# A stack of position-mixing convolutions: fp32 matmuls replaced by products of float32r pieces

## The chip, the cores and the metric

The kernel runs on one core of one Trainium2 chip. The metric is the device time of one execution in microseconds (us); the time of before is the median of three runs. The core has TensorE (PE; its weight loads are listed apart as PEld), VectorE (DVE), ScalarE (ACT), GpSimd (POOL) and SyncE (SP). SP and ACT issue the DMAs here, each in the order of its own queue.

## The reference

A float32 image `x` of shape (4, 32, 32, 16) (batch, height, width, channel) passes through four layers, each added to its input. Layers 0 to 2 are one function with different weights:

```python
def layer(inputs, M, Wp, G):              # inputs = group_norm(x)
    first = einsum('ijpq,bpqc->bijc', M2, inputs)
    shifted = conv3x3(inputs, K)          # K: G as [3, 3, c, (h, w, f)]: own taps for each position (i, j)
    diff = relu(inputs[:, :, :, None, None, :] - shifted)
    second = einsum('ijpq,bpqijc->bijc', W2, diff)
    return first - second
```

For each of the 1024 positions (i, j) a 3x3 convolution of the whole image with 16 input and 16 output channels is computed, subtracted from the image, clipped at zero and summed over the image with the weights `Wp` of that position. Layer 3 is a causal two-dimensional convolution whose impulse response is the inverse DFT of a quotient of two DFTs, made from 8x8 coefficients.

## The kernel before

**Layout.** A position is (cc, p, q) with row 8 cc + p and column q. The pair (cc, q) is a "blk", 128 of them; the eight p and 16 channels make up the 128 partitions. One blk's convolution is a matmul whose 128 outputs are (p, f), whose contraction is (tap, input channel), and whose 512 columns are half of one batch's image. Four batches of 32 x 32 columns are therefore eight such matmuls, taken four at a time (two batches, two halves): the loop `for b0 in (0, 2)` inside `for blk in range(NBLK)`, 256 groups a layer and 768 in all.

**Taps.** The image is normalised (`group_norm`, L82), padded into `ypad`, written to DRAM (`img`, L125, eight DMAs) and read back twelve times with a shift for each tap (`load_patches`, L118; copies on L135). `main` holds taps 0 to 7 on 8 x 16 partitions, so eight taps are one K = 128 matmul (L226). `last` holds tap 8 four times, on 16 partitions of each of the four row tiles of the array, so that the four matmuls of the ninth tap (L235, K = 16) work in four row tiles on four PSUM banks. Everything is fp32.

**Second term.** VectorE reads two PSUM banks at a time, takes the minimum with 0, multiplies by `Wp` and sums along the row in one instruction (L244), two for each group.

**Loads.** `load_g` (L179, ACT's queue) brings G for eight blks at a time (a chunk, 16 a layer): 512 KB for eight taps and four copies of the ninth tap's 64 KB; POOL subtracts the identity at the centre tap (L193). `load_w` (L201, SP's queue) brings 1 MB of Wp for two blks. `load_m` (L141) brings M in four parts of 1 MB for the first term (`first_term`, L146: transposes, 64 matmuls of 64 columns on L159, transposes back).

**PSUM.** Two pools: `ps`, three tiles of two banks for the groups, and `sm`, two single banks for everything else.

**Impulse response.** `impulse_response` (L259) is a generator; layer 0 takes one step of it after each blk (`next(side, None)`), so that its matmuls (L280, L281, L316), its POOL arithmetic (L293 to L304) and its loads lie between the groups of layer 0. Layer 3 then uses the result (L377).

A planner orders each engine's instructions by the dependences and an estimate of when they are ready; each engine runs its own list in order. In the order of before, half of layer 1's and layer 2's first term comes after the first groups of the loop.

Of the kernel before, what the change touches and what calls it, by code (L numbers as in the profile page):

```python
"""Three preactivated position-mixing convolutions and a causal IIR convolution on a (4, 32, 32, 16) image.

Positions.  A position n = (cc * 8 + p) * 32 + q is split into p (8 values) and blk = (cc, q) (128
values).  The residual stream lives in SBUF as [(p, channel), batch, blk].

Layers 0 to 2.  Per position n, s - y is a 3x3 convolution of the normalised image y with
G[n] - (1 at the centre tap).  TensorE computes it for the 8 x 16 (p, f) of a blk at a time, on an image
that holds each tap's shifted copy on partitions of its own: eight taps are one K = 128 matmul, and
the ninth is a K = 16 matmul in one of four row tiles of the array, which work side by side on four
PSUM banks.  VectorE then computes sum_m Wp[n, m] * min(s - y, 0) in one pass over PSUM.  # L10

Layer 3.  The filter's impulse response comes from DFTs as matmuls; the truncated linear
convolution is a block-Toeplitz matmul over (row in block, channel), one for each shift in q and
each block of eight rows, all accumulated in one PSUM bank.
"""
# [8 lines left out]
F32 = mybir.dt.float32  # L24
AF = mybir.ActivationFunctionType
# [8 lines left out]
ROW = B * 34  # one padded image row of all batches  # L34
IMG = 34 * ROW
SPAN = 31 * ROW + 3 * 34 + 32  # what a tap's copy has to hold
GC = 8  # blks per load of G
# [4 lines left out]
TQ = 4  # shifts in q per load of the Toeplitz operand  # L42
# [3 lines left out]
def conv_stack_kernel(ctx, tc, x, M, W, G, den, num, h0, cst, dft, idft, out):  # L46
# [7 lines left out]
    wp = ctx.enter_context(tc.tile_pool(name="wp", bufs=3))  # L54
    gp = ctx.enter_context(tc.tile_pool(name="gp", bufs=2))
    mp = ctx.enter_context(tc.tile_pool(name="mp", bufs=2))
    junkp = ctx.enter_context(tc.tile_pool(name="junk", bufs=2))
    tp = ctx.enter_context(tc.tile_pool(name="tp", bufs=3))
    dram = ctx.enter_context(tc.tile_pool(name="dram", bufs=1, space=DRAM))
    ps = ctx.enter_context(tc.tile_pool(name="ps", bufs=3, space=PSUM))  # L60
    sm = ctx.enter_context(tc.tile_pool(name="sm", bufs=2, space=PSUM))

    def small_psum():
        return sm.tile([P, 512], F32, tag="sm", name="sm")

# [6 lines left out]
    # normalised image with zero columns at the sides, and the zero rows of its copy in DRAM  # L72
    ypad = const.tile([P, 4, B, 34], F32, name="ypad")
    nc.gpsimd.memset(ypad, 0.0)
    zrow = const.tile([C, ROW], F32, name="zrow")
    nc.gpsimd.memset(zrow, 0.0)
    img = dram.tile([C, 34, ROW], F32, name="img")
    nc.scalar.dma_start(out=img[:, 0, :], in_=zrow)
    nc.scalar.dma_start(out=img[:, 33, :], in_=zrow)
    hd = dram.tile([C, C, HLEN], F32, name="hd")  # L80

    def group_norm(xt):  # L82
        """(x - mean) / sqrt(var + 1e-5) over positions and pairs of channels."""
# [18 lines left out]
        # ScalarE's root is short of fp32: one step of Heron's rule after it  # L102
# [15 lines left out]
    def load_patches(y):  # L118
        """[(tap, channel), row, batch, column] of taps 0 to 7, and tap 8 four times over."""
        nc.vector.tensor_copy(  # L120
            ypad[:, :, :, 1:33], y.rearrange("p b (cc q) -> p cc b q", q=S)
        )
        rows = img[:, 1:33, :].rearrange("c (cc p) x -> p c cc x", p=8)
        for p in range(8):
            (nc.sync, nc.scalar)[p % 2].dma_start(  # L125
                out=rows[p],
                in_=ypad[p * C : (p + 1) * C].rearrange("c cc b x -> c cc (b x)"),
            )
        flat = img.rearrange("c r x -> c (r x)")
        main = pp.tile([P, 34, B, 34], F32, tag="main", name="main")  # L130
        last = pp.tile([P, 34, B, 34], F32, tag="last", name="last")
        jobs = [(main, t * C, (t // 3) * ROW + t % 3) for t in range(8)]
        jobs += [(last, g * 32, 2 * ROW + 2) for g in range(4)]
        for n, (to, at, shift) in enumerate(jobs):
            (nc.sync, nc.scalar)[n % 2].dma_start(  # L135
                out=to[at : at + C].rearrange("c r b x -> c (r b x)")[:, :SPAN],
                in_=flat[:, shift : shift + SPAN],
            )
        return main, last

    def load_m(layer, part):  # L141
        mt = mp.tile([P, 2, 8, P], F32, tag="mt", name="mt")
        nc.scalar.dma_start(out=mt, in_=M[layer][:, 2 * part : 2 * part + 2])
        return mt

    def first_term(layer, xt, y):  # L146
        """x + M y, as [(p, c), b, blk]."""
# [6 lines left out]
        for part in range(4):  # L154
            mt = load_m(layer, part)
            for k in range(2):
                pn = 2 * part + k
                for pm in range(8):
                    nc.tensor.matmul(  # L159
                        pf[:, bass.ts(pn, B * C)],  # L160
                        lhsT=mt[:, k, pm, :],
                        rhs=yt[:, pm].rearrange("k b c -> k (b c)"),
                        start=(pm == 0),
                        stop=(pm == 7),
                    )
# [13 lines left out]
    def load_g(layer, ch):  # L179
        g = gp.tile([P, GC, 8, C], F32, tag="g", name="g")  # L180
        g9 = gp.tile([P, GC, 8, C], F32, tag="g9", name="g9")
        cols = bass.ts(ch, GC * P)
        nc.scalar.dma_start(
            out=g.rearrange("r n p f -> r (n p f)"), in_=G[layer][:P, cols]
        )
        for t in range(4):
            nc.scalar.dma_start(
                out=g9[32 * t : 32 * t + C].rearrange("r n p f -> r (n p f)"),
                in_=G[layer][P : P + C, cols],
            )  # L190
        # the centre tap gives s - y in place of s
        mid = g[64 : 64 + C].rearrange("r n p f -> r (n p) f")
        nc.gpsimd.tensor_tensor(  # L193
            mid,
            mid,
            ident[64 : 64 + C, 64 : 64 + C].unsqueeze(1).to_broadcast([C, GC * 8, C]),
            ALU.subtract,
        )
        return g, g9

    def load_w(layer, blk):  # L201
        """Wp's rows of two blks, each on its 16 partitions."""
# [9 lines left out]
    def conv_layer(layer, xt, side=None):  # L212
        y = group_norm(xt)
        main, last = load_patches(y)
        xf = first_term(layer, xt, y)
        acc = work.tile([P, B, NBLK], F32, tag="acc", name="acc")
        for blk in range(NBLK):
            if blk % GC == 0:
                g, g9 = load_g(layer, blk // GC)
            if blk % 2 == 0:  # L220
                wt = load_w(layer, blk)
            n = blk % GC
            for b0 in (0, 2):
                pt = [ps.tile([P, 2, 512], F32, tag="pt", name="pt") for _ in range(2)]
                for t in range(4):
                    nc.tensor.matmul(  # L226
                        pt[t // 2][:, t % 2, :],
                        lhsT=g[:, n].rearrange("r p f -> r (p f)"),
                        rhs=main[:, bass.ts(t % 2, 16), b0 + t // 2, :S],
                        start=True,  # L230
                        stop=False,
                    )
                for t in range(4):
                    rows = slice(32 * t, 32 * t + C)
                    nc.tensor.matmul(  # L235
                        pt[t // 2][:, t % 2, :],
                        lhsT=g9[rows, n].rearrange("r p f -> r (p f)"),
                        rhs=last[rows, bass.ts(t % 2, 16), b0 + t // 2, :S],
                        start=False,
                        stop=True,  # L240
                    )
                for t in range(2):
                    junk = junkp.tile([P, S * S], F32, tag="junk", name="junk")
                    nc.vector.scalar_tensor_tensor(  # L244
                        junk,
                        pt[t].rearrange("p h m -> p (h m)"),
                        0.0,
                        wt[:, blk % 2, :],
                        ALU.min,
                        ALU.mult,  # L250
                        accum_out=acc[:, b0 + t, blk : blk + 1],
                    )
            if side is not None:
                next(side, None)
# [83 lines left out]
    def load_toeplitz(k):  # L338
# [3 lines left out]
        for p in range(8):  # L342
# [3 lines left out]
            )  # L346
        return t

    xs = conv_layer(0, xs, impulse_response())
    xs = conv_layer(1, xs)  # L350
    xs = conv_layer(2, xs)

# [102 lines left out]
```

## Time and profile before

| | us |
|---|---|
| three runs | 3991.12, 3995.35, 4002.98 |
| median | 3995.35 |
| profiled execution, span | 3994.8 |
| TensorE busy | 3884.4 (97%) |
| VectorE busy | 1863.0 (47%) |
| ScalarE busy | 15.3 |
| GpSimd busy | 154.1 |
| DMA | 281.95 MB, mean 71 GB/s |
| mean granted TensorE clock | 0.984 |

Busy times are unions over the span: TensorE's matmuls overlap in its pipeline, so their mean duration (612 ns for a record of L226) is longer than the time from one to the next. In the groups of instructions each line reads: line, engine, operation, output<-inputs, shapes and count; then busy us and the mean ns of one; then the idle time just before them on that engine and what ended most of it. In a timeline a line is: start, duration, engine, line, operation, count, and in brackets the idle time before and what ended it. In a table of stretches each row is the stretch, then busy us (and count) of PE, PEld, DVE, ACT and POOL, the granted TensorE clock, the DMA engines' share and GB/s.

### The profile page before, as it was taken

The page shows a single profiled execution, that of the slowest core. Times are in us where ns is not written, and L with a number is a line of the kernel's source. Part 1 is how long each engine was busy: PE and PEld are TensorE (multiplying, and loading weights), DVE is VectorE, ACT ScalarE, POOL GpSimd, SP SyncE. Part 2 cuts the span into 40 slices and gives each one's busy share as a digit, 9 for nine tenths or more (in the row PEclk, how much of TensorE's full clock was granted, in tenths as well). Part 3 has the DMA queues.
Part 4 walks back from the last instruction along what each step waited for, and adds up shares of the span by engine and source line. Part 5 has one row for each costly group of instructions (what it writes and reads, how often), then busy time and mean ns, then how long its engine had stood idle before and what let it go on. Part 6 is the DMA issues. An engine that isn't in the chain of part 4 may idle for free.

```text
span 3994.8 us, 32173 instructions
## 1 busy us (share of the span) xinstructions
PE 3884.4 (97%) x13092; PEld 1490.9 (37%) x13092; DVE 1863.0 (47%) x3137; ACT 15.3 (0%) x27; POOL 154.1 (4%) x112
## 2 busy tenths in 40 slices
PE   4999999999999899999999999979999999999998
PEld 3333333333333333333333333343333333333335
DVE  0444444444444444444444444434444444444441
ACT  0000000000000000000000000000000000000000
POOL 0300000000000000000000000000000000000000
PEclk9999999999999899999999999979999999999999
DMA  6235322222223432222222222252222222222214
GB/s 157 59 77 104 78 61 69 66 66 69 61 65 74 79 96 66 61 67 67 66 62 69 63 67 71 61 97 61 61 69 67 65 61 69 65 66 70 61 43 69
DMA packets 65186, 281.95 MB, mean 71 GB/s; under 512 B 8173, under 2 KB 26381, under 8 KB 38350
## 3 DMA queue, kind: packets, MB, share of 16 engines
q1 hardware_dynamic: 39806, 218.72, 23.6%
q10 hardware_dynamic: 25232, 61.17, 6.4%
q8 instruction: 102, 1.67, 0.2%
q14 instruction: 46, 0.38, 0.0%
HBM read 277.43 MB, written 2.43 MB: 70 GB/s over the span
## 4 chain that ended last, share of the span: by engine, by line
PE 96%; DMA 4%; DVE 0%; issue 0%; POOL 0%; SPq 0%; ACT 0%; ACTq 0%; POOLq 0%; DVEq 0%
PE pt L226 71%; PE pt L235 21%; PE sm L377 2%; DMA last<-img 1%; DMA w<-in_W_dram 1%; PE sm L316 1%; PE sm L159 1%; DMA table<-in_dft_dram 1%; DMA main<-img 0%; DMA tb<-in_idft_dram 0%; PE sm L280 0%; DVE junk L244 0%; PE sm L281 0%; DMA g<-in_G_dram 0%; DMA img<-ypad 0%
## 5 line engine op out<-in xcount | busy, mean ns | idle before, releaser
L226 PE MATMUL pt<-main,g 128*128 128x512 f32 x6144 | 2888.2, 612 | 48.1 <-DMA last<-img 47.9
L244 DVE SCALAR_TENSOR_TENSOR junk<-pt,w 128x1024 f32<-128x1024 f32 x1536 | 1819.8, 1222 | 2010.5 <-PE pt L235 2010.5
L226 PEld LDWEIGHTS pt<-main,g 128*128 128x128 f32 x6144 | 1105.1, 190 | 1769.2 <-issue 1584.4
L235 PE MATMUL pt<-last,g 16*128 16x512 f32 x6144 | 904.5, 645 | 0.0
L235 PEld LDWEIGHTS pt<-last,g 16*128 16x128 f32 x6144 | 243.4, 183 | 603.8 <-issue 574.0
L193 POOL TENSOR_TENSOR g<-g,cs 16x1024 f32<-16x1024 f32 x48 | 112.5, 2344 | 3537.1 <-DMA g<-in_G_dram 3388.6
L244 DVE DVE_READ_ACCUMULATOR junk<-pt,w 128x1 f32 x1536 | 127.0, 83 | 0.0
L159 PE MATMUL sm<-yt,mt 128*128 128x64 f32 x384 | 70.0, 371 | 21.7 <-ACT yt L152 21.7
L159 PEld LDWEIGHTS sm<-yt,mt 128*128 128x128 f32 x384 | 69.0, 283 | 26.2 <-ACT yt L152 22.9
L377 PE MATMUL sm<-t,y 128*128 128x512 f32 (+3 forms) x256 | 72.3, 447 | 1.5 <-DVE y L357 1.5
L377 PEld LDWEIGHTS sm<-t,y 128*128 128x128 f32 x256 | 45.1, 197 | 28.8 <-issue 17.0
L316 PE MATMUL sm<-tb,H 128*128 128x512 f32 (+1 forms) x80 | 37.9, 616 | 0.0
L384 DVE TENSOR_TENSOR xo<-xo,sm 128x512 f32<-128x512 f32 x1 | 0.7, 686 | 72.4 <-PE sm L377 72.4
L316 PEld LDWEIGHTS sm<-tb,H 128*128 128x128 f32 (+1 forms) x80 | 14.6, 190 | 21.8 <-issue 21.8
L87 PE MATMUL sm<-s,cs 128*128 128x4 f32 x8 | 2.3, 361 | 16.4 <-DVE s L85 16.4
L297 DVE RECIPROCAL d<-d 128x256 f32<-128x256 f32 (+1 forms) x5 | 8.8, 1750 | 16.2 <-POOL d L296 16.2
L99 PE MATMUL sm<-ss,cs 128*128 128x4 f32 x8 | 2.3, 362 | 11.7 <-DVE ss L97 11.7
L150 PE MATMUL sm<-cs,y 128*128 128x128 f32 x12 | 3.3, 433 | 6.7 <-DVE y L113 6.7
L104 ACT ACTIVATE r<-v 128x4 f32<-128x4 f32 x4 | 0.8, 204 | 2243.8 <-DVE v L101 2243.8
L174 DVE TENSOR_TENSOR xf<-x,sm 128x512 f32<-128x512 f32 x3 | 2.1, 687 | 15.8 <-PE sm L170 15.8
L87 PEld LDWEIGHTS sm<-s,cs 128*128 128x128 f32 x8 | 2.0, 311 | 18.9 <-DVE s L85 14.1
L293 POOL TENSOR_TENSOR t<-sb,sa 128x256 f32<-128x256 f32 (+1 forms) x10 | 7.2, 723 | 0.4
(50 smaller groups left out, 106.0 us busy)
## 6 DMA issues: line engine op xcount, KB each, us to landing
w<-in_W_dram SPq DMA_DIRECT2D x192, 1024.0 KB
g<-in_G_dram ACTq DMA_DIRECT2D x48, 512.0 KB
mt<-in_M_dram ACTq DMA_DIRECT2D x12, 1024.0 KB
g<-in_G_dram ACTq DMA_DIRECT2D x192, 64.0 KB
t<-hd SPq DMA_DIRECT2D x32, 160.0 KB
t<-hd ACTq DMA_DIRECT2D x32, 160.0 KB
tb<-in_idft_dram SPq DMA_DIRECT2D x16, 256.0 KB
main<-img ACTq DMA_DIRECT2D x12, 271.9 KB
```

The lines of the kernel that those rows point to most:

```text
L87: nc.tensor.matmul(pm[:, :B], lhsT=avg, rhs=s, start=True, stop=True)
L99: nc.tensor.matmul(pv[:, :B], lhsT=avg, rhs=ss, start=True, stop=True)
L150: nc.tensor.transpose(py[:, bass.ts(b, P)], y[:, b, :], ident)
L159: nc.tensor.matmul(pf[:, bass.ts(pn, B * C)], lhsT=mt[:, k, pm, :], rhs=yt[:, pm].rearrange("k b c -> k (b c)"), start=(pm == 0), stop=(pm ...
L193: nc.gpsimd.tensor_tensor(mid, mid, ident[64 : 64 + C, 64 : 64 + C].unsqueeze(1).to_broadcast([C, GC * 8, C]), ALU.subtract,)
L226: nc.tensor.matmul(pt[t // 2][:, t % 2, :], lhsT=g[:, n].rearrange("r p f -> r (p f)"), rhs=main[:, bass.ts(t % 2, 16), b0 + t // 2, :S], ...
L235: nc.tensor.matmul(pt[t // 2][:, t % 2, :], lhsT=g9[rows, n].rearrange("r p f -> r (p f)"), rhs=last[rows, bass.ts(t % 2, 16), b0 + t // 2 ...
L244: nc.vector.scalar_tensor_tensor(junk, pt[t].rearrange("p h m -> p (h m)"), 0.0, wt[:, blk % 2, :], ALU.min, ALU.mult, accum_out=acc[:, b0 ...
L293: mul = lambda o, u, w: nc.gpsimd.tensor_tensor(o, u, w, ALU.mult)
L297: nc.vector.reciprocal(d, d)
L316: nc.tensor.matmul(ph[ij], lhsT=H[:nf, ch, ri, bass.ts(ij, P)], rhs=tb[:nf], start=(ch == 0 and ri == 0), stop=(ch == len(FCH) - 1 and ri ...
L377: nc.tensor.matmul(pov[:, :, 8 * cc :], lhsT=y3[:, cc, 31 - dq : 31 - dq + S, :].rearrange("p q b -> p (q b)"), rhs=t[:, :, q * PITCH : q ...
```

## The change

- **Pieces.** The image and G are each split into two float32r tensors, a high part (the value rounded by a copy to float32r) and a low part (the value less the high part). The image's are made on VectorE (`ypad` gets a second plane), G's on ACT (high) and VectorE (low).
- **Products.** The eight taps are four products (high x high, high x low, low x high, low x low), each one float32r matmul of 512 columns: 16 matmuls for a group in place of four fp32 ones (`main_taps`).
- **Ninth tap.** Its four products are stacked along the contraction: 64 rows, 16 for each product, twice over on the 128 partitions (`gn`, and `last` with high and low alternating). Its matmul is K = 64 in one of two row tiles (`last_tap`).
- **Order.** A group is now called a job. Jobs are taken in pairs: the main taps of one, the ninth tap of both, the main taps of the other. In the first chunk of a layer all eight blks go with the first two batches, then with the other two.
- **Image.** It is written for each part and each pair of batches: `img` is [part, pair, c, row, 2 x 34]; 32 DMAs write it and 48 read it back.
- **G.** A chunk is loaded and split one chunk ahead (`next_g`); the raw tiles have one buffer, the pieces two. The ninth tap is loaded eight times in place of four.
- **M** comes in eight parts with three buffers in place of four with two. **Wp** has four buffers in place of three.
- **PSUM.** One pool, four tiles of two banks, for everything.
- **Impulse response.** All of it runs ahead of layer 0's loop (`for _ in side: pass`).

The core of the diff:

```diff
-    ypad = const.tile([P, 4, B, 34], F32, name="ypad")
+    ypad = const.tile([P, 2, 4, B, 34], F32R, name="ypad")
...
+        hi, lo = ypad[:, 0, :, :, 1:33], ypad[:, 1, :, :, 1:33]
+        nc.vector.tensor_copy(hi, yv)
+        nc.vector.tensor_tensor(lo, yv, hi.bitcast(F32), ALU.subtract)
...
+        for pair in range(2):
+            for h in range(2):
+                for p in range(8):
+                    (nc.sync, nc.scalar)[n % 2].dma_start(
+                        out=rows[h, pair, p],
...
+            for k in range(8):
+                shift = 2 * ROW + 2
+                (nc.sync, nc.scalar)[n % 2].dma_start(
+                    out=last[k * C : (k + 1) * C, pair]
...
+        gh = gs.tile([P, GC, P], F32R, tag="gh", name="gh")
+        gl = gs.tile([P, GC, P], F32R, tag="gl", name="gl")
+        gn = gs.tile([P, GC, P], F32R, tag="gn", name="gn")
+        nc.scalar.copy(gh, g)
+        nc.vector.tensor_tensor(gl, g, gh.bitcast(F32), ALU.subtract)
+        nc.scalar.copy(gn, g9)
+        for r in (32, 96):
+            lo = gn[r : r + 32]
+            nc.vector.tensor_tensor(lo, g9[r : r + 32], lo.bitcast(F32), ALU.subtract)
...
+        def main_taps(job, tiles, start):
+            blk, a = job
+            for w in range(2):
+                for h in range(2):
+                    for t in range(4):
+                        nc.tensor.matmul(
+                            tiles[t // 2][:, t % 2, :],
+                            lhsT=gt[layer, blk // GC][w][:, blk % GC, :],
+                            rhs=main[h][:, a, bass.ts(t % 2, 16), t // 2, :S],
+                            start=start and w == 0 and h == 0,
+                            stop=not start and w == 1 and h == 1,
+                        )
...
+        def last_tap(job, tiles, start):
+            blk, a = job
+            for t in range(4):
+                rows = slice(64 * (t % 2), 64 * (t % 2) + 64)
+                nc.tensor.matmul(
+                    tiles[t // 2][:, t % 2, :],
+                    lhsT=gt[layer, blk // GC][2][rows, blk % GC, :],
+                    rhs=last[rows, a, bass.ts(t % 2, 16), t // 2, :S],
+                    start=start,
+                    stop=not start,
+                )
...
+        for one, two in zip(jobs[::2], jobs[1::2]):
+            for blk, _ in (one, two):
+                if blk % GC == 2:
+                    next_g(layer, blk // GC + 1)
+                if blk // 2 not in wt:
+                    wt[blk // 2] = load_w(layer, blk // 2 * 2)
+            p1 = [pair_psum() for _ in range(2)]
+            main_taps(one, p1, True)
+            p2 = [pair_psum() for _ in range(2)]
+            last_tap(one, p1, False)
+            last_tap(two, p2, True)
+            main_taps(two, p2, False)
+            second_term(one, p1)
+            second_term(two, p2)
```

In the changed program main taps stand on L277, the ninth tap on L289, the second term on L301, the first term on L192, the split of G on L234 to L239, the image's writes on L140 and its copies on L158 and L167, the impulse response's matmuls on L350, L351 and L386.

## The prediction

> **What bounds the kernel now.** I read the chain of waits first, then the groups of instructions, then the timeline of a steady stretch, and last the timeline and the stretches around a layer's start.
>
> ```profile
> PE 96%; DMA 4%; DVE 0%; issue 0%; POOL 0%; SPq 0%; ACT 0%; ACTq 0%; POOLq 0%; DVEq 0%
> ...
> L226 PE MATMUL pt<-main,g 128*128 128x512 f32 x6144 | 2888.2, 612 | 48.1 <-DMA last<-img 47.9
> L244 DVE SCALAR_TENSOR_TENSOR junk<-pt,w 128x1024 f32<-128x1024 f32 x1536 | 1819.8, 1222 | 2010.5 <-PE pt L235 2010.5
> L226 PEld LDWEIGHTS pt<-main,g 128*128 128x128 f32 x6144 | 1105.1, 190 | 1769.2 <-issue 1584.4
> L235 PE MATMUL pt<-last,g 16*128 16x512 f32 x6144 | 904.5, 645 | 0.0
> ```
>
> TensorE is 96% of the chain, and VectorE waits 2010.5 us for it, so VectorE is cover and not bound. The source issues 3072 matmuls on L226 and as many on L235; the trace has 6144 records of each. One fp32 matmul is therefore two records.
>
> ```profile
> 1001.28 0.19 PEld L226 LDWEIGHTS pt<-main,g 128*128 128x128 f32 x1 [0.24 <-issue]
> ...
> 1003.45 0.19 PEld L226 LDWEIGHTS pt<-main,g 128*128 128x128 f32 x1 [0.25 <-issue]
> 1004.42 0.31 PEld L235 LDWEIGHTS pt<-last,g 16*128 16x128 f32 x8 [0.78 <-issue]
> 1004.42 1.17 PE L235 MATMUL pt<-last,g 16*128 16x512 f32 x8
> 1005.51 0.30 PEld L226 LDWEIGHTS pt<-main,g 128*128 128x128 f32 x2 [0.78 <-issue]
> 1005.51 3.75 PE L226 MATMUL pt<-main,g 128*128 128x512 f32 x8
> ```
>
> Five records pass between the loads at 1001.28 and 1003.45: 0.434 us a record. The group repeats every 4.77 us (1004.42 to the next at 1009.19): 8 x 0.434 = 3.47 main, two records' time for the ninth tap (its four row tiles run side by side) = 0.87, and 0.43 left over for two changes between full array and row tiles, 0.215 each. 768 such groups are 3663 us of the 3994.8.
>
> ```profile
> 1374.80 3.39 ACTq L125 DMA_DIRECT2D img<-ypad  x4
> 1378.23 0.58 ACT L152 COPY yt<-sm 128x512 f32<-128x512 f32 x1 [5.67 <-DMA img<-ypad]
> 1378.87 13.91 PE L159 MATMUL sm<-yt,mt 128*128 128x64 f32 x64 [3.39 <-ACT yt L152]
> 1379.72 1.85 ACTq L135 DMA_DIRECT2D main<-img  x4
> ...
> 1394.49 25.11 ACTq L143 DMA_DIRECT2D mt<-in_M_dram  x3
> 1402.07 6.35 PE L226 MATMUL pt<-main,g 128*128 128x512 f32 x10 [9.29 <-DMA last<-img]
> ...
> 1415.45 3.79 PE L159 MATMUL sm<-yt,mt 128*128 128x64 f32 x32
> ```
>
> Between layers TensorE stops at 1363.3 and starts convolving at 1402.1: 38.8 us, ended by the image's copies. The yt copy goes ahead of the copies' issue on ACT's queue, and half of the first term runs later, inside the loop.
>
> ```profile
> 45.00:67.00 22.00, 0.07 (x1) 0.10 (x1) 0.00 (x0) 0.00 (x0) 0.00 (x0) 1.00 1.04 161
> ...
> 1380.00:1394.00 14.00, 12.79 (x60) 12.60 (x60) 0.00 (x0) 0.00 (x0) 0.00 (x0) 0.50 1.02 140
> ```
>
> The last two columns are the DMA engines' busy share and GB/s: while patches load, the DMA engines are full at 140 to 161 GB/s.
>
> **Price of a one-pass matmul.** No row of before has float32r. Upper bound: as much as a whole fp32 record, 0.434. Lower bound: half a record, 0.217. The four widths on L377 take 12.6, 19.5, 26.6 and 34.6 us for 64 records each, about 0.11 us for each 128 columns, so a record's time is its columns, streamed more than once; a product that streams them half as often is half a record. What could hold it above that is its own weight load, one per matmul as now. A load lasts 0.19, but loads overlap: 32 records of 64 columns on L159 pass in 3.79 us, 0.118 each, load included. That is below 0.217, so I take 0.217. The Trainium skill (TensorE: Matmul & The Clock Gate, "Back-to-back issue gap" and "LDWEIGHTS") gives 215.7 ns for 512 columns in one pass and an estimate of 107 ns for a 128-column load; the sum by it is the same within 1%. The same page's section on fast weight load speaks against the change in one point, that four-byte weights get no faster load; no run here shows it for float32r.
>
> **The loop.** Main taps: 16 x 0.217 = 3.47 a job, against 8 x 0.434 = 3.47: nothing gained. Ninth tap: four K=64 matmuls in two row tiles, two abreast: 2 x 0.217 = 0.43 against 0.87. Mode changes: two per two jobs: 0.215 a job against 0.43. A job is 4.12 against 4.77, so 0.65 x 768 = 499 us less; a layer is 256 x 4.12 = 1055.
>
> VectorE's second term keeps its 2 x 1.15 us a job (0.82 to 1.97 of a pair in the timeline), 4.6 in a pair's 8.24. Split work is added to it: per chunk of G (48 chunks, eight pairs each) a 128x1024 subtraction and two 32x1024 ones, 1.22 us each by twice the 128x512 row (0.69) less its fixed part, 3.7 in all. The schedule of after puts the two small ones ahead of a pair's third tile and the large one ahead of its fourth. The pair then ends on VectorE about 4.4 us after TensorE, and the fourth tile is wanted again 4.1 after: 0 to 0.4 us a chunk, 0 to 20, taken as 10. ACT's two 128x1024 copies a chunk (near 1.1 each by its 0.58 for 128x512) stand beside 66 us of matmuls, and G's loads go out a chunk ahead; without that cover the 1 MB (near 7 us) would stand before each chunk, 340 in all. POOL's 2.34 us correction is hidden as now.
>
> **Starts of layers 1 and 2.** Now SP and ACT issue 32 image writes instead of 8 and 48 copies of 139 KB instead of 12 of 278 KB, and the yt copy stands behind all of ACT's share; the first term, with the whole of M, stands in PE's order ahead of the loop. From the last convolution matmul: 11.0 to y (1363.3 to 1374.3 now), 1.1 for the two copies into ypad, 14 for the writes (between 6.9 + 3.2 = 10, issue at 0.43 each and one landing, and four rounds of today's 4.9 = 20, since in the changed program's schedule each issue waits for the DMA eight before it), then 6.7 MB at 150 GB/s = 45, of which the last eight copies (7.4) need not land before yt. yt is issued at about 64. Then the first term: 128 records at the 0.217 of the cold 64 (13.91) are 28; with five of eight M tiles loaded only now (2.6 MB, 17 us, beside them) about 26 from yt, and 1.7 for ft and its transposes: 91. A layer takes 91 + 1055 = 1146. Now layer 1 runs 1363.3 to 2634.6 and layer 2 to 3908.1: 1271 and 1273.5, with the half first term and the cold start inside. So 125 and 127.5 less. Ends: gap 70 with DMA at 196 GB/s (the first 25 us) and the short write time, 120 with 20 for writes and M in series.
>
> A rule that speaks against this step: the Trainium skill (DMA: Bandwidth & Descriptors, "Specifications") wants 512 B and more per piece for full rate. The rows written to the image shrink from 544 to 272 B. The trace has no such write; by the rule 0.56 MB would go slower by a few us a layer, which is inside 10 to 20.
>
> **Layer 0.** Ahead of the patches now go four W tiles, four of the inverse DFT, 1 MB of G and 1.5 MB of M, some 8.4 MB: 52 us at 160 GB/s. Writes and copies as above bring yt to about 105, the first term (with 3 MB of M and G behind it) to 127. Then the impulse response stands in series, no longer between groups: five steps of POOL at 8 us (eleven operations of 0.61 to 0.73) and its G correction, 45; then four matmuls and the second half of the inverse DFT, 24 x 0.87 = 21. The loop starts at about 190 (155 to 225) against 66.9, and ends at 1245 against 1363.3: 118 less, as the loop now holds 75 us of these matmuls besides its groups.
>
> **Sum.** The last layer and the end (3908.1 to 3994.8) stay. 3994.8 - 118 - 125 - 127.5 + 10 = 3634, taken as 3635 us. The profiled execution is 0.6 us below the runs' median of 3995.35, so nothing is added.
>
> **Rivals.** (1) Slower: the pitch of a float32r matmul is above 0.217, its load not hidden or its passes not one. Place: L277 and L289, 18 pitches a job, 13,824 in all. My gain of 360 is used up at 360 / 13,824 = 0.026 more, a pitch of 0.243. With the load starting 0.10 after its predecessor and lasting 0.19 as in the steady rows, 0.29: 13,824 x 0.073 = 1009 more, 4640 us. At a whole record, 0.434: 6635. For it: no row shows float32r, and the margin is small. Against it: 0.118 on L159. Chance 0.12. (2) The starts of layers cost more: with DMAs waiting for those eight before, gaps of 130 and a layer 0 loop start at 240 give 3635 + 78 + 50 = 3765, still faster. For it: the DMA engines are full there; against: it needs both ends at once. 0.11. (3) The changes of mode vanish behind the loads and the starts are at their short ends: 3635 - 165 - 77 = 3395 at most, 3500 if half of it comes. For it: nothing in the rows; 0.05. (4) VectorE becomes the bound: 4.6 + 3.7/8 = 5.1 of 8.24 a pair; it would need 60% more work. Not given a chance of its own.
>
> **Numbers.** Forecast 0.72, own range 3540 to 3740 (starts -77 to +93, VectorE +-10, 0.1 us a job either way for the mode changes = 77). With (2) and (3), 3500 to 3790; only (1) and the far ends are left out. A difference of 0.3%, 12 us, is what the runs of before (3991 to 4003) can tell. Faster 0.87, the same 0.01, slower 0.12.
>
> **What would show it.** A record of L277 every 0.217 us, as many records as matmuls (16 x 768 = 12,288 there); pairs every 8.24; L289 at about 0.87 + 0.2 a pair; the yt copy at 64 us after the last matmul, the loop at 91; layer 0's loop at 190; VectorE under 60%. It is wrong if the pitch is above 0.24, or if TensorE waits within the loop for VectorE or G.

## The result and the profile after

The changed kernel takes 4121.21 us (median of 4 runs, 4115.94 to 4123.3) against 3999.16 us for the kernel before in the same comparison (4 runs, 3991.12 to 4004.68). The ratio is 1.0303, with an interval of 1.0286 to 1.0319: slower, where 3635 us was forecast. The profiled execution spans 4119.0 us.

These lines are from the page of the changed kernel: the chain of waits, and the groups of TensorE, its weight loads and VectorE's second term (total busy, mean ns of one, idle before).

```profile
PE 92%; DMA 5%; POOL 1%; DVE 1%; SPq 0%; issue 0%; ACT 0%; ACTq 0%; DVEq 0%; POOLq 0%
...
L301 DVE SCALAR_TENSOR_TENSOR junk<-pt,w 128x1024 f32<-128x1024 f32 x1536 | 1880.7, 1224 | 1598.7 <-PE pt L289 888.0
L277 PE MATMUL pt<-main,gh 128*128 128x512 f32 x6144 | 1721.0, 423 | 0.0
L277 PE MATMUL pt<-main,gl 128*128 128x512 f32 x6144 | 1667.0, 415 | 0.0
L277 PEld LDWEIGHTS pt<-main,gh 128*128 128x128 f32 x6144 | 1143.1, 191 | 471.4 <-issue 152.9
...
L289 PE MATMUL pt<-last,gn 64*128 64x512 f32 x3072 | 486.1, 436 | 0.0
```

TensorE still sets the end, and VectorE still waits for it. L277 has 12,288 records for 12,288 matmuls, so a float32r matmul is one record where an fp32 one was two. The mean of one (423 and 415 ns) is the length of its record, and records overlap; what counts is the distance from one start to the next, the pitch. It is read from a steady stretch of the timeline (start, duration, engine, line, what, how many):

```profile
1006.08 1.27 PE L289 MATMUL pt<-last,gn 64*128 64x512 f32 x8
1007.27 2.29 PE L277 MATMUL pt<-main,gh 128*128 128x512 f32 x8
1009.40 2.17 PE L277 MATMUL pt<-main,gl 128*128 128x512 f32 x8
1011.40 2.19 PE L277 MATMUL pt<-main,gh 128*128 128x512 f32 x8
1013.42 2.17 PE L277 MATMUL pt<-main,gl 128*128 128x512 f32 x8
1015.52 1.27 PE L289 MATMUL pt<-last,gn 64*128 64x512 f32 x8
```

A pair of jobs goes from one ninth tap to the next: 1006.08 to 1015.52, 9.44 us where 8.24 was forecast. Eight matmuls of L277 take about 2.0 us, not 1.74. The starts of the single records, averaged over all steady runs of 32 matmuls, show that the four row-halves t of a product are not alike:

```
matmul reads            batch (t // 2)   rows start at      pitch, ns (changed kernel)
t = 0                   first            a multiple of 16 B    240
t = 1                   first            a multiple of 16 B    232
t = 2                   second           8 B past one          264
t = 3                   second           8 B past one          272
mean of all                                                    251.5
```

A row of the image is two batches of 34 floats. The first batch starts on a multiple of 272 B and the second 136 B behind it, and 136 is 8 more than a multiple of 16. The matmuls of the second batch are 0.03 us dearer. That is a hint and no proof: the two batches also write different PSUM tiles. The experiments separate these.

The start of layer 1, again from the timeline of the changed kernel, ACT with its queue first and then TensorE, whose last convolution matmul of layer 0 ends at 1417.5:

```profile
1431.09 9.24 ACTq L140 DMA_DIRECT2D img<-ypad  x16
1440.50 11.50 ACTq L158 DMA_DIRECT2D main<-img  x8
1452.66 7.39 ACTq L167 DMA_DIRECT2D last<-img  x4
1460.76 15.69 ACTq L158 DMA_DIRECT2D main<-img  x8
1477.09 7.29 ACTq L167 DMA_DIRECT2D last<-img  x4
1484.42 0.58 ACT L187 COPY yt<-pt 128x512 f32<-128x512 f32 x1 [55.57 <-DMA last<-img]
...
1485.06 27.57 PE L192 MATMUL pt<-yt,mt 128*128 128x64 f32 x128 [53.23 <-ACT yt L187]
1513.30 1.12 PE L203 MATMUL pt<-cs,ft 128*128 128x128 f32 x4 [0.68 <-ACT ft L200]
1514.07 2.48 PE L277 MATMUL pt<-main,gh 128*128 128x512 f32 x5
```

The yt copy stands in ACT's queue behind all of ACT's DMA issues, and TensorE waits 53 us for it. The gap is 96.6 us here and 98.1 us at layer 2, where it was 38.7 and 41.0.

Where the difference from the forecast lies, in three terms that can be read off the timeline. Loops of the three layers: 1209.7, 1210.5 and 1210.0, together 3630 against 3 x 1055 = 3165, so +465. Starts: 207.8 against 190, and gaps of 96.6 and 98.1 against 91 each, +31. The 10 us allowed for VectorE did not come. 465 + 31 - 10 = 486, and 4119 - 3634 is 485.

### The profile page after: what moved, and what is told of

It is laid out like the page before. It is cut to its first block, busy times and chain, and to the rows that moved or that the text cites. A ratio compares the mean times of both kernels' runs of the same rounds, so it can differ in the third digit from the quotient of the medians.

```text
span 4119.0 us, 39252 instructions
## 1 busy us (share of the span) xinstructions
PE 3858.6 (94%) x16164; PEld 2740.8 (67%) x16164; DVE 2102.4 (51%) x3284; ACT 117.0 (3%) x124; POOL 158.7 (4%) x112
## 4 chain that ended last, share of the span: by engine, by line
PE 92%; DMA 5%; POOL 1%; DVE 1%; SPq 0%; issue 0%; ACT 0%; ACTq 0%; DVEq 0%; POOLq 0%
PE pt L277 77%; PE pt L289 11%; DMA main<-img 2%; PE pt L449 2%; DMA w<-in_W_dram 2%; PE pt L192 2%; DMA last<-img 1%; PE pt L386 1%; SPq L140 0%; POOL t L363 0%; DVE junk L301 0%; POOL H L363 0%; DMA mt<-in_M_dram 0%; DMA g<-in_G_dram 0%; DVE gn L239 0%
## 5 line engine op out<-in xcount | busy, mean ns | idle before, releaser
L301 DVE SCALAR_TENSOR_TENSOR junk<-pt,w 128x1024 f32<-128x1024 f32 x1536 | 1880.7, 1224 | 1598.7 <-PE pt L289 888.0
L277 PE MATMUL pt<-main,gh 128*128 128x512 f32 x6144 | 1721.0, 423 | 0.0
L277 PE MATMUL pt<-main,gl 128*128 128x512 f32 x6144 | 1667.0, 415 | 0.0
L277 PEld LDWEIGHTS pt<-main,gh 128*128 128x128 f32 x6144 | 1143.1, 191 | 471.4 <-issue 152.9
L277 PEld LDWEIGHTS pt<-main,gl 128*128 128x128 f32 x6144 | 1174.2, 191 | 368.9
L289 PE MATMUL pt<-last,gn 64*128 64x512 f32 x3072 | 486.1, 436 | 0.0
L289 PEld LDWEIGHTS pt<-last,gn 64*128 64x128 f32 x3072 | 261.1, 186 | 210.8 <-issue 165.5
L192 PE MATMUL pt<-yt,mt 128*128 128x64 f32 x384 | 83.0, 422 | 185.4 <-ACT yt L187 181.1
L192 PEld LDWEIGHTS pt<-yt,mt 128*128 128x128 f32 x384 | 82.2, 333 | 186.8 <-ACT yt L187 182.3
L301 DVE DVE_READ_ACCUMULATOR junk<-pt,w 128x1 f32 x1536 | 127.7, 83 | 0.0
L239 DVE TENSOR_TENSOR gn<-g,gn 32x1024 fp32r<-32x1024 f32 x96 | 117.6, 1225 | 8.6 <-ACT gn L236 5.7
L449 PE MATMUL pt<-t,y 128*128 128x512 f32 (+3 forms) x256 | 72.1, 446 | 1.5 <-DVE y L428 1.5
L234 ACT CAST gh<-g 128x1024 fp32r<-128x1024 f32 x48 | 50.5, 1051 | 55.3 <-PE pt L277 55.3
L386 PE MATMUL pt<-tb,H 128*128 128x512 f32 (+1 forms) x80 | 40.6, 669 | 8.5 <-ACT sa L356 4.9
L386 PEld LDWEIGHTS pt<-tb,H 128*128 128x128 f32 (+1 forms) x80 | 16.5, 212 | 32.6 <-issue 20.4
```

Of the source, the lines that this page charges most:

```text
L192: nc.tensor.matmul(pf[:, bass.ts(pn, B * C)], lhsT=mt[:, pm, :], rhs=yt[:, pm].rearrange("k b c -> k (b c)"), start=(pm == 0), stop=(pm == 7),
L234: nc.scalar.copy(gh, g)
L239: nc.vector.tensor_tensor(lo, g9[r : r + 32], lo.bitcast(F32), ALU.subtract)
L277: nc.tensor.matmul(tiles[t // 2][:, t % 2, :], lhsT=gt[layer, blk // GC][w][:, blk % GC, :], rhs=main[h][:, a, bass.ts(t % 2, 16), t // 2, ...
L289: nc.tensor.matmul(tiles[t // 2][:, t % 2, :], lhsT=gt[layer, blk // GC][2][rows, blk % GC, :], rhs=last[rows, a, bass.ts(t % 2, 16), t // ...
L301: nc.vector.scalar_tensor_tensor(junk, tiles[t].rearrange("p h m -> p (h m)"), 0.0, wt[blk // 2][:, blk % 2, :], ALU.min, ALU.mult, accum_ ...
```

## The experiments

The theory after the result was: a float32r matmul streams its rows more slowly when they start off a 16-byte boundary, and that, not the weight load, keeps the pitch above 0.243. The rivals: the weight load, which no longer fits under a short matmul; the breaks between rows of 32 columns; and an intrinsic price of float32r.

**Rows of 36 columns.** Each batch's row becomes 144 B, a multiple of 16, and the tiles keep 32 rows in place of 34; nothing else changes.

```diff
-ROW = 2 * 34
+ROW = 2 * 36
-SPAN = 31 * ROW + 34 + 32
+SPAN = 31 * ROW + 36 + 32
-    ypad = const.tile([P, 2, 4, B, 34], F32R, name="ypad")
+    ypad = const.tile([P, 2, 4, B, 36], F32R, name="ypad")
-            pp.tile([P, 2, 34, 2, 34], F32R, tag=f"main{h}", name=f"main{h}") for h in range(2)
+            pp.tile([P, 2, 32, 2, 36], F32R, tag=f"main{h}", name=f"main{h}") for h in range(2)
-        last = pp.tile([P, 2, 34, 2, 34], F32R, tag="last", name="last")
+        last = pp.tile([P, 2, 32, 2, 36], F32R, tag="last", name="last")
```

> Image rows are padded to 36 columns in place of 34, so that the rows of both batches of a pair start on 16 bytes (row start theory). In the changed kernel the matmuls on the first batch (t = 0, 1) pass every 0.235 us and those on the second (t = 2, 3), whose rows start 8 bytes off, every 0.270. Row start theory: all four at 0.235, a pair of jobs 36 x 0.235 + 0.36 = 8.82 us in place of 9.38, and 384 x 0.56 = 215 us less: 3905. Weight load theory (each one-pass matmul shows part of its own load of 0.19): pitch stays at 0.25, time stays at 4120. PSUM theory (t = 2, 3 write the other PSUM tile): 0.235 and 0.270 stay, 4120.

3854.8 us (3853.32 to 3857.44), ratio to before 0.9632 (0.9615 to 0.9648). The timeline of this run at the same kind of place:

```profile
2006.05 1.20 PE L289 MATMUL pt<-last,gn 64*128 64x512 f32 x8
2007.18 2.12 PE L277 MATMUL pt<-main,gh 128*128 128x512 f32 x8
2009.14 2.02 PE L277 MATMUL pt<-main,gl 128*128 128x512 f32 x8
2011.00 2.02 PE L277 MATMUL pt<-main,gh 128*128 128x512 f32 x8
2012.85 2.02 PE L277 MATMUL pt<-main,gl 128*128 128x512 f32 x8
2014.80 1.20 PE L289 MATMUL pt<-last,gn 64*128 64x512 f32 x8
```

A pair is 8.75 instead of 9.44, and eight matmuls take 1.86 instead of 2.0. The mean pitch is 0.2316, and the four t lie between 0.227 and 0.238: the second batch costs what the first does, though it still writes another PSUM tile. Two floats of padding turn "slower by 3%" into "faster by 3.7%". The time fell by 266 us where 215 were expected, as the old pair is 9.44 and not 9.38, and the aligned pitch 0.2316 and not 0.235. Still, 0.2316 is not the forecast 0.217.

**No breaks between rows.** Each matmul reads 512 columns in one piece (other columns of the image than the layer needs).

```diff
-                            rhs=main[h][:, a, bass.ts(t % 2, 16), t // 2, :S],
+                            rhs=main[h][:, a].rearrange("p r b x -> p (r b x)")[:, bass.ts(t, 512)],
```

(The ninth tap likewise.)

> The moving operands are 512 contiguous columns, on 16 bytes, in place of 16 rows of 32: the matmuls multiply other columns of the image. Row start theory: all four pitches equal and no longer than 0.235; if each row costs something by itself, 0.217, a pair at 36 x 0.217 + 0.36 = 8.17 us and about 3655 in all. Weight load theory: 0.25 as before. PSUM theory: 0.235 and 0.270 still alternate.

3853.2 us in one run, mean pitch 0.2316. One piece of 2048 B or sixteen aligned pieces of 128 B makes no difference, so breaks between aligned rows cost nothing that shows, and what lies between 0.2316 and 0.217 does not come from them.

**A shorter weight load.** The two cross products (high with low) load 96 of 128 weight columns.

```diff
+                    m = P if w == h else 96
-                            tiles[t // 2][:, t % 2, :],
-                            lhsT=gt[layer, blk // GC][w][:, blk % GC, :],
+                            tiles[t // 2][:m, t % 2, :],
+                            lhsT=gt[layer, blk // GC][w][:, blk % GC, :m],
```

> The products high x low and low x high use 96 of the 128 weight columns, so 32 output rows lack these two products; the other two products stay at 128. Weight load theory: the load is a quarter shorter (0.19 to 0.14), and the pitch of these eight of sixteen matmuls falls by up to 0.05, to about 0.217 in the mean: some 150 us less in all. Row start and PSUM theories: 0.235 and 0.270 in all groups, 4120 in all.

4111.2 us in one run. From this run's page, the loads of L277 (here L278, the file being a line longer):

```profile
L278 PEld LDWEIGHTS pt<-main,gl 128*96 128x96 f32 (+1 forms) x6144 | 1093.6, 178 | 472.2
L278 PEld LDWEIGHTS pt<-main,gh 128*128 128x128 f32 (+1 forms) x6144 | 1057.4, 177 | 521.1 <-issue 152.9
```

The mean load falls from 191 to 177 or 178 ns, as it must when half the loads are shorter; the mean pitch goes from 0.2515 to 0.2505. A load bound would have followed the load. This rival falls; the run with fewer columns below speaks against it too, as its matmuls pass every 0.175 us with full loads.

**fp32 for the main taps, float32r for the ninth tap alone.** The main taps go back to one fp32 product of raw image and raw weights; the stacked ninth tap and the paired mode changes stay.

```diff
-            for w in range(2):
-                for h in range(2):
-                    for t in range(4):
...
-                            lhsT=gt[layer, blk // GC][w][:, blk % GC, :],
-                            rhs=main[h][:, a, bass.ts(t % 2, 16), t // 2, :S],
...
+            for t in range(4):
+                nc.tensor.matmul(
+                    tiles[t // 2][:, t % 2, :],
+                    lhsT=gt[layer, blk // GC][0][:, blk % GC, :],
+                    rhs=main[:, a, bass.ts(t % 2, 16), t // 2, :S],
+                    start=start,
+                    stop=not start,
+                )
```

(The image gets a third plane with the raw values, and the split of G's main taps goes.)

> The main taps go back to one fp32 matmul (two records of 0.434), the ninth tap stays split with two jobs per mode change. If only the main taps' pitch went wrong: a job is 8 x 0.434 + (9.38 - 8.02) / 2 = 4.15 us against 4.69, 768 x 0.54 = 415 us less, and 16 of 48 copies of the image fewer at each start, about 10 us each: 3675. If the ninth tap's part brings nothing either, a job is at the old 4.77 and the time about 4120 + 60 = 4180.

3648.2 us (3646.73 to 3651.08), ratio 0.9115 (0.9101 to 0.9128). Its timeline:

```profile
2002.22 1.26 PE L280 MATMUL pt<-last,gn 64*128 64x512 f32 x8
2003.41 7.22 PE L268 MATMUL pt<-main,g 128*128 128x512 f32 x16
2010.56 1.26 PE L280 MATMUL pt<-last,gn 64*128 64x512 f32 x8
```

A pair is 8.34, close to the 8.24 that was forecast for the change itself. So most of the forecast's gain is real, and it comes from the ninth tap and the mode changes, not from the main taps, which were costed at "nothing gained". fp32 records here pass in 0.429 (first batch) and 0.440 us (second): fp32 feels the 8 bytes too, but by 0.011 a record, not 0.03.

**The same with rows of 36 columns**, the edit of the first experiment on the one above.

> The run with fp32 main taps, with image rows padded to 36 columns. Its fp32 records pass every 0.429 us on the first batch and every 0.440 on the second. Row start theory: 0.429 for all, 8 x 0.0055 = 0.044 us a job, 34 us less: 3614. If fp32 does not care for the row start and the 0.011 comes from elsewhere: 3648 as before.

3595.89 us (3592.1 to 3602.72), ratio 0.8979 (0.8964 to 0.8994). A pair is 8.19, and the records of both batches pass in 0.429. The pair fell by 0.15, of which the main records make 8 x 0.011 = 0.09; the rest lies around the ninth tap, whose float32r rows are aligned now as well. The expectation had left that out.

**The order of a layer's start.** On the version above, the first term is traced ahead of the image's loads, the loads of M go out on POOL's queue, and the copies of the impulse response go from ACT to VectorE.

```diff
-        nc.scalar.dma_start(out=mt, in_=M[layer][:, part])
+        nc.gpsimd.dma_start(out=mt, in_=M[layer][:, part])
...
-                nc.scalar.copy(sa[:nf], pa[:nf].rearrange("p (r n) -> p r n", r=2))
-                nc.scalar.copy(sb[:nf], pb[:nf].rearrange("p (r n) -> p r n", r=2))
+                nc.vector.tensor_copy(sa[:nf], pa[:nf].rearrange("p (r n) -> p r n", r=2))
+                nc.vector.tensor_copy(sb[:nf], pb[:nf].rearrange("p (r n) -> p r n", r=2))
```

(`main, last = load_patches(y)` moves behind the call of `first_term`.)

> The same with another start of a layer: the first term stands ahead of the image's copies in the program, M is issued by POOL in place of ACT, and the two copies of the impulse response's sums go to VectorE. If the starts of layers cost what the queues' order makes them cost (yt and M behind all patches): gaps between layers fall from 85 to about 60 us, the first loop starts at about 130 in place of 186, and 105 us go: 3510. If the DMA engines' rate alone sets the starts (the same bytes, at 150 GB/s): at most 10 us each, about 3590.

3495.83 us (3492.06 to 3499.36), ratio 0.8732 (0.8719 to 0.8745), the fastest version of this study. Layer 0's loop starts at 141.7 instead of 194.1, and the gaps are 56.1 and 54.3 instead of 86.8 and 87.8.

**These three edits alone on the changed kernel.**

> The changed kernel with nothing else than the other start of a layer (first term ahead of the copies, M issued by POOL, the impulse response's two copies on VectorE). With fp32 main taps this took 100 us off (first loop 194 to 142, gaps 87 to 56). Here 16 more copies of the image a layer have to land, of which eight before the loop. If the queues' order sets the starts: 90 to 100 less, 4025. If the DMA rate does: under 50 less, 4075 or more.

4010.04 us (10 runs, 4002.04 to 4015.07), ratio to before 1.0027 (1.0009 to 1.0044): 111 less than the changed kernel. Layer 0's loop starts at 155.0, the gaps are 61.2 and 58.5. The start of layer 1 in this run, ACT first and then TensorE; the last convolution matmul ends at 1363.3:

```profile
1377.67 0.59 ACT L187 COPY yt<-pt 128x512 f32<-128x512 f32 x1 [3.01 <-PE pt L185]
...
1378.31 20.75 PE L192 MATMUL pt<-yt,mt 128*128 128x64 f32 x96 [0.68 <-ACT yt L187]
1399.32 7.09 PE L192 MATMUL pt<-yt,mt 128*128 128x64 f32 x32 [0.27 <-DMA mt<-in_M_dram]
1407.08 1.12 PE L203 MATMUL pt<-cs,ft 128*128 128x128 f32 x4 [0.68 <-ACT ft L200]
1424.52 4.07 PE L277 MATMUL pt<-main,gh 128*128 128x512 f32 x8 [16.33 <-DMA last<-img]
```

The yt copy comes 14 us after the last matmul instead of 67, and the first term runs while the image is copied. Now it is the image's last copies that end the gap. Moving three things in the queues saves 111 us of the 122 that the whole change lost, with no byte less to move. The first loop's start and the two gaps were 402 us together in the changed kernel, 147 before and 275 here: the moves took back 128 of the 256 us by which the starts had grown, and the loops are 10 us longer. So which engine issues what, and in which order, made about half of the longer starts. What each of the three moves did was not tried, and the other half holds, among other things, work that the kernel before did inside its loops.

**One mode change more per job.** On the first experiment's version, each job runs its own main taps and its own ninth tap.

```diff
-            last_tap(two, p2, True)
-            main_taps(two, p2, False)
+            main_taps(two, p2, True)
+            last_tap(two, p2, False)
```

> The float32r kernel with rows padded to 36, but with main taps and ninth tap of one job, then of the other: two mode changes a job in place of one. By the 0.215 us a change read from the kernel before: 768 x 0.215 = 165 us more than 3855, 4020. If the changes cost only what a pair of jobs leaves over beside its 36 pitches (0.36 for two changes): 138 more, 3993. If they hide behind weight loads: 3855.

4046.9 us in one run. Its timeline:

```profile
2000.27 2.12 PE L277 MATMUL pt<-main,gh 128*128 128x512 f32 x8
2002.23 2.02 PE L277 MATMUL pt<-main,gl 128*128 128x512 f32 x8
2004.18 0.74 PE L289 MATMUL pt<-last,gn 64*128 64x512 f32 x4
2004.84 2.12 PE L277 MATMUL pt<-main,gh 128*128 128x512 f32 x8
```

A single job is 4.57 in steady rows and 4.61 on average, 9.22 a pair instead of 8.74. The three loops are 181 us longer together for 768 more changes: 0.24 us a change. The steady rows alone give (2 x 4.57 - 8.74) / 2 = 0.20. The 0.215 read from the kernel before lies between the two.

**Fewer columns.** On the first experiment's version, the cross products stream 384 of 512 columns.

```diff
+                    R = 16 if w == h else 12
-                            tiles[t // 2][:, t % 2, :],
+                            tiles[t // 2][:, t % 2, : 32 * R],
-                            rhs=main[h][:, a, bass.ts(t % 2, 16), t // 2, :S],
+                            rhs=main[h][:, a, 16 * (t % 2) : 16 * (t % 2) + R, t // 2, :S],
```

> The float32r kernel with rows padded to 36; in the products high x low and low x high each matmul streams 12 of 16 rows, 384 of 512 columns, so a quarter of the image lacks these two products. What is left of the pitch above 0.2145 (0.2315 at 512 columns) is either a slower rate per column (384 columns: 0.174), a fixed cost beside 0.417 ns a column (0.178), or a floor of another kind such as the weight load (stays near 0.23). The time falls by 6144 x 0.053 = about 325 us in the first two cases, to 3530, and not at all in the third.

3541.4 us in one run. Its timeline, from one ninth tap to the next (main taps here on L278, the ninth tap on L290):

```profile
2000.53 1.20 PE L290 MATMUL pt<-last,gn 64*128 64x512 f32 x8
...
2008.36 0.97 PE L290 MATMUL pt<-last,gn 64*128 64x512 f32 x6
```

A pair is 7.83 instead of 8.74, 0.057 us less for each of its 16 shorter matmuls. Inside a run of matmuls, those of 384 columns pass in 0.170 to 0.182, about 0.175 us, and those of 512 in 0.231 as before. (0.2315 - 0.175) / 128 = 0.44 ns a column, and 512 x 0.44 leaves some 0.006 us fixed. fp32 has 0.429 a record; counted as two passes of 512, which no run shows directly, that is 0.419 ns a column and pass. So the 0.017 us by which an aligned float32r matmul exceeds half an fp32 record looks mostly like a slower rate for each column, not a fixed cost per matmul: a fixed 0.017 would have given 0.178 at 384 columns, and that is only 0.003 off. Why it is slower is open. A floor near 0.23, by the load or anything else, is ruled out.

**Every row off the boundary.** On the first experiment's version, the main taps read from a later column: 4 B for the high part of the image, 8 B for the low part, in both batches.

```diff
-SPAN = 31 * ROW + 36 + 32
+SPAN = 31 * ROW + 36 + 34
-                            rhs=main[h][:, a, bass.ts(t % 2, 16), t // 2, :S],
+                            rhs=main[h][:, a, bass.ts(t % 2, 16), t // 2, h + 1 : h + 1 + S],
```

> The float32r kernel with rows padded to 36, and the moving rows of the main taps read from one column later (4 bytes, high part of the image) or two (8 bytes, low part): the matmuls multiply a shifted image. Row start theory, in the form that a row of 128 bytes which starts off 16 bytes touches nine 16-byte pieces in place of eight: all main taps at 0.270 for both offsets, 12,288 x 0.0385 = 473 us more than 3855, 4330. If only 8 bytes off costs, as seen so far: half of it, 4090. If it was the batch or the PSUM tile after all: 3855.

4180.9 us in one run. Its timeline:

```profile
2003.89 1.19 PE L289 MATMUL pt<-last,gn 64*128 64x512 f32 x8
2005.01 2.33 PE L277 MATMUL pt<-main,gh 128*128 128x512 f32 x8
2007.17 2.23 PE L277 MATMUL pt<-main,gl 128*128 128x512 f32 x8
2009.24 2.23 PE L277 MATMUL pt<-main,gh 128*128 128x512 f32 x8
2011.31 2.23 PE L277 MATMUL pt<-main,gl 128*128 128x512 f32 x8
2013.47 0.73 PE L289 MATMUL pt<-last,gn 64*128 64x512 f32 x4
```

Eight matmuls take 2.07 us, the mean pitch is 0.2583, and it is alike for all four t and for both offsets. 12,288 x (0.2583 - 0.2316) = 328, and the run is 326 us longer than the aligned one. So alignment is the cause, with the layout's strides, banks and loads unchanged. The size was expected higher: 0.2583 is not the 0.264 to 0.272 of the second batch in the changed kernel.

A row of 128 B touches eight sixteen-byte pieces when aligned and nine when not, by 4 or by 8 B. Nine to eight is 1.125; 0.2583 to 0.2316 is 1.115. The Trainium skill (SBUF — State Buffer, "Specifications (TRN2)") says that the memory is read in lines of 16 bytes and that each step to a new line is paid for. It gives no amount; a pitch that went by the number of pieces would agree with the aligned and the shifted run within 1%. The second batch of the changed kernel lies above that, 0.268 to the first batch's 0.236, 1.14, and fp32 far below it, 0.440 to 0.429, 1.03. That pieces are what is counted is therefore a guess; that alignment moves the float32r pitch is shown.

**fp32 for the ninth tap too**, on the version with fp32 main taps and 36 columns: four row tiles of K=16 again, still paired.

```diff
-        last = pp.tile([P, 2, 32, 2, 36], F32R, tag="last", name="last")
+        last = pp.tile([P, 2, 32, 2, 36], F32, tag="last", name="last")
...
-                rows = slice(64 * (t % 2), 64 * (t % 2) + 64)
+                rows = slice(32 * t, 32 * t + C)
```

> The run with fp32 main taps and rows of 36, and its ninth tap in fp32 too (K = 16 in four row tiles, as before the change), still two jobs a mode change; the split of G's ninth tap is left out. If stacking four float32r products on 64 rows is what halves the ninth tap: a pair needs 4 x 0.434 = 1.74 us there in place of 4 x 0.2315 = 0.93, 384 x 0.81 = 311 us more than 3596, 3907, which leaves the paired mode changes (about 180) and the padding as all that is gained on the kernel before. If the ninth tap's gain is the paired change alone: 3596.

3895.35 us in one run, 299 above the version with float32r there. Its timeline (main taps here on L262, the ninth tap on L274):

```profile
2001.03 2.00 PE L274 MATMUL pt<-last,g 16*128 16x512 f32 x16
2002.96 7.13 PE L262 MATMUL pt<-main,g 128*128 128x512 f32 x16
2010.03 2.00 PE L274 MATMUL pt<-last,g 16*128 16x512 f32 x16
```

A pair is 8.99 instead of 8.19, 384 x 0.8 = 307. Putting the four products of the ninth tap one above the other on 64 rows about halves its time, and these 300 us are what float32r is worth in this kernel.

## Why the prediction was wrong, point by point

**The step that failed is the price of a one-pass matmul**, "half a record, 0.217". The changed kernel's pitch is 0.2515 on average, above the 0.24 that the prediction itself named as a sign of being wrong. 13,824 x (0.2515 - 0.217) = 477 us, against 465 by which the loops were longer than forecast; the few us the other way are mode changes a little cheaper than the 0.215 taken (a pair leaves 9.44 - 36 x 0.2515 = 0.39 for two). The 0.0345 has two parts. 0.0199 is alignment: the padded version has 0.2316, 13,824 x 0.0199 = 275, and it measured 266 less. The other 0.0146 (some 200 us) stays in every float32r run with 512 columns, the one without breaks between rows included; it looks like a slower rate per column, and its cause is open. The prediction priced a form that no row showed by the bare count of passes. It asked whether the load could hold the pitch up, but never where the rows start. The trace of the kernel before holds a faint sign of it, in the lines left out between the two loads that the prediction quoted (the weight loads of L226, one for each record):

```profile
1001.71 0.19 PEld L226 LDWEIGHTS pt<-main,g 128*128 128x128 f32 x1 [0.24 <-issue]
...
1002.56 0.19 PEld L226 LDWEIGHTS pt<-main,g 128*128 128x128 f32 x1 [0.24 <-issue]
1003.01 0.19 PEld L226 LDWEIGHTS pt<-main,g 128*128 128x128 f32 x1 [0.25 <-issue]
1003.45 0.19 PEld L226 LDWEIGHTS pt<-main,g 128*128 128x128 f32 x1 [0.25 <-issue]
```

From 1001.71 to 1002.56 two records pass in 0.85, from 1002.56 to 1003.45 two pass in 0.89: the first batch's 0.429 and the second's 0.440. The prediction averaged them to 0.434 over five records, and so lost the one row that told the batches apart.

The Trainium skill (TensorE: Matmul & The Clock Gate, "Back-to-back issue gap"), which the prediction set beside its 0.217, gives N / 2.4 + 2.5 ns for a matmul by itself when warm, 215.8 for 512 columns, and about 131 ns for each of a stream of loads and matmuls. No float32r run here reached either at 512 columns, the lowest mean pitch being 231.6 ns. The measurement decides.

**Rival 1 came true in its arithmetic and not in its mechanism.** Its break-even, a pitch of 0.243, held on both sides: 0.2515 was slower than before and 0.2316 faster. Its cause, a load that is not hidden at 0.29, did not: with shorter loads the pitch stayed (0.2505).

**Main taps: "nothing gained".** The direction was worse than that. Four float32r matmuls at 0.2515 are 1.006 us where two fp32 records at 0.434 are 0.868.

**The ninth tap and the mode changes** were right in their mechanism. The fp32 main version has a pair of 8.34 (8.24 forecast). The ninth tap alone was worth 299 by the last experiment against 768 x 0.43 = 330 forecast, its two pitches a job being priced at the same 0.217; a change is 0.20 to 0.24 by the single-job run against 0.215.

**VectorE as cover** held: it is busy for 51% of the span, and its waits in the layer loop are for TensorE. The 10 us allowed for the split did not show.

**Starts of layers 1 and 2.** The yt copy was forecast 64 us after the last matmul and came at 67; the loop was forecast at 91 and came at 96.6 and 98.1. The reading (the copy stands behind ACT's share of the image) was right, and the start-only run agrees with it: with the first term ahead of the image's loads the copy comes at 14.

**Layer 0.** Its loop was forecast at 190 (155 to 225) and starts at 207.8, inside the bounds; these 18 us and the gaps are the other, small part of the miss.

**The range.** 3500 to 3790 left out rival 1, at a chance of 0.12. The margin was 0.026 us on 0.217, 12%, on the one price in the sum that no row supported; "0.118 on L159" bounds the load but says nothing of how float32r streams its rows.

## What to carry to other kernels

A price that is multiplied by 13,824 and stands in no row needs its own bounds, lay-out included: look where each moving row starts, and pad rows to a multiple of 16 bytes before a float32r matmul is judged. Replacing one fp32 product by four float32r products gained nothing on a full array, aligned or not (4 x 0.2316 = 0.926 against two records' 0.858); here it paid only where the extra products went on rows that stood idle, as in the ninth tap. When a change gives an engine's queue more to issue at a stage's start, move the one instruction that everything waits for ahead of it; here three moves together were worth 111 us.

## What the runs showed of the hardware that was not expected

An aligned float32r matmul of 512 columns passes in 0.2316 us, while an fp32 matmul passes in two records of 0.429 each; a float32r matmul is dearer than half such a record by 8%.

Float32r is sensitive to where its moving rows start (0.2316 aligned, 0.2583 with all rows off by 4 or 8 B), and fp32 hardly (0.429 and 0.440 a record). When aligned and unaligned matmuls alternate two by two, the unaligned ones took 0.264 to 0.272, more than in a run of unaligned ones alone; the distance between rows differs there too (272 B, and 288 B in the shifted run), and no run here tells which it is.

In the start-only run ACT issues no image write from 1388.5 to 1406.4, because the copy of the first term's result stands in its queue and waits for TensorE, and then the image's last copies end the gap. Putting that copy on another engine was not tried.
